# Joining the third and last layers of a graph network in one loop of fixed order, and moving half of an input check into the attention layer

## Chip, cores, metric

One core of one Trainium2 chip. The metric is device time in microseconds (us) of one execution; lower is better. Engines are PE (TensorE matmul; PEld its weight loads), DVE (VectorE), ACT (ScalarE), POOL (GpSimd) and SP (SyncE, which here only issues transfers). A name such as L935 is a line of the kernel whose profile is shown; the same statement has other line numbers in each kernel.

## The reference, cut to what matters

Four layers on 4096 nodes with 128 features, each followed by a residual sum and a layer norm. All use one 4096 x 4096 fp32 adjacency, 64 MB, of zeros and ones.

```python
x = layernorm(x + L0(x, adj, ...))   # hyperbolic graph convolution
x = layernorm(x + L1(x, adj, ...))   # attention with 4 heads, masked by adj == 0
x = layernorm(x + L2(x, adj, w2))    # relu(D^-1/2 (adj + I) D^-1/2 @ x @ w2)
x = layernorm(x + L3(x, adj, ...))   # additive attention:
#   H = X W^T + b ; e = leaky_relu(A * H a_s + A * (H a_r)^T, 0.2)
#   softmax over A > 0, times H
```

L1 is called **layer one** here and in the prediction, L2 the **third layer**, L3 the **last layer**. The change's own summary ("layer two") counts from one and means layer one by that name.

The last layer has two versions. The fast one splits exp(leaky_relu(s + r)) into factors, which is valid only if the adjacency holds nothing but 0 and 1 and the scores are not too large. So the kernel **searches** the whole adjacency for any other value: `(a != 0) != a`, summed into `odd`. A flag made from that sum chooses the branch.

## The kernel before: the parts concerned

An adjacency block `adjT[I, J]` is 1 MB (128 partitions x 2048 fp32): column tile I, row group J, NS = 8 of each. Layer one takes 32 steps (`jb`) per tile. In a step PE makes scores, ACT their exponentials, DVE masks them (`e`), and PE multiplies them by the values (`pv`) two steps later. Meanwhile pieces of the previous tile's `ending` run between the steps. ACT also reads the adjacency rows in halves, for the degrees.

```python
# layer one, rot is a pool with one buffer
def row(n):                                         # ACT issues the load of the next half row
    st["nat"] = rot.tile([P, N // 2], F32, tag="nat", name="nat")
    nc.scalar.dma_start(out=st["nat"], in_=self.adj[...])
def degree():                                       # ACT sums the half row, then loads the next
    nc.scalar.activation(nat, nat, AF.Identity, accum_out=self.deg2[:, k, i : i + 1])
    row(n + 1)
for n in range(-LEAD, len(seq)):                    # fixed order on every engine
    if n + LEAD < len(seq):
        if jb % 4 == 3 and ...: degree()
        scores(I, jb)                               # PE ps, ACT exp, DVE e
    if n >= 0:
        sums(I, jb)                                 # PE pv
        next(rest, None)                            # one piece ("bit") of the previous ending

# third layer
at2 = ctx.enter_context(tc.tile_pool(name="at2", bufs=8))
for I in range(NS):
    for J in range(NS):
        at = at2.tile([P, 4, S], F32, tag="at", name="at")
        (nc.scalar if J % 2 else nc.sync).dma_start(out=at, in_=self.adjT[I, J])
        for jb in range(4): nc.tensor.matmul(pa, lhsT=Y[:, 4 * J + jb, :], rhs=at[:, jb, :], ...)
        nc.vector.scalar_tensor_tensor(odd, at, 0.0, at, op0=ALU.not_equal, op1=ALU.not_equal,
                                       accum_out=self.odd[...])       # the search
    # product with w2, relu, residual, layer norm of the tile

# last layer: preparation (transposes, scores, row sums, flag), then the branch, then
#   exponentials, F, X + bias, and eight tiles: DVE makes w, PE multiplies F by it
```

## Time and profile before

| | us |
|---|---|
| Whole kernel, median (range of 3) | 2355.86 (2355.78 to 2356.20) |
| Layer one, start of the first pv to start of the last | 1026.8 to 1805.6 = 778.8 |
| Last pv to the third layer's first matmul (pa) | 7.8, then 8.55 of waiting after one group |
| Third layer, first to last pa | 244.5 |
| Preparation of the last layer and the branch | 50.0 |
| Last layer, first to last pa | 235.6 |

The prediction below shows the busy shares, the stretches and the chain. The waits of PE complete them (engine, its work and line, what it waited for; then us in total, how often, longest us):

```profile
PE pa L1345 <- DVE w L1342: 12.4, 1, 12.4
...
PE pa L1200 <- DMA at<-adjT: 8.6, 1, 8.6
...
PE ps L912 <- ACT e L919: 2.7, 4, 1.8
...
PE pv L938 <- DVE e L921: 1.8, 2, 1.0
```

The first line is the wait behind the branch, the second the one at the third layer's start. The last two are all that layer one's 779 us have of PE waiting: PE sets its pace.

### The profile page before, as it was taken

To read this page: it belongs to the slowest core of one execution; us is meant where nothing else is said; L and a number is where in the kernel's file an instruction comes from. 1 tells how busy PE (TensorE), PEld (TensorE's weight loads), DVE (VectorE), ACT (ScalarE), POOL (GpSimd) and SP (SyncE) were. 2 spreads that over 40 slices of the span, in tenths; PEclk is the share of its full clock that TensorE was granted. 3 is DMA by queue.
4 is the path that set the end of the run, shared out by engine and by line. 5 is a ranking of instruction groups with operands and counts; after the bars stand their busy time and mean duration, and the time that the engine had idled before them with its cause. 6 is when DMAs were issued, how large, how long until landed. Compare 5 with 4: busy or idle time off the path is not lost.

```text
span 2354.3 us, 24080 instructions
## 1 busy us (share of the span) xinstructions
PE 2013.7 (86%) x8795; PEld 1118.5 (48%) x8795; DVE 1896.6 (81%) x2708; ACT 1463.7 (62%) x1777; POOL 106.9 (5%) x146
## 2 busy tenths in 40 slices
PE   4478878777787772589999999999998999979998
PEld 4266666666665662353333333333333444444443
DVE  6488888888878788877888888888877877579887
ACT  5688898988988987558787888878875000010000
POOL 2000000000000015212000000000000000000000
PEclk7689889989888896689999999999999999979999
DMA  2455565555646450488665655556554877438884
GB/s 54 127 191 180 169 204 191 182 184 168 223 142 214 160 180 9 134 241 230 184 194 179 190 176 188 182 176 197 179 182 171 329 286 285 160 139 291 293 291 165
DMA packets 112868, 448.44 MB, mean 190 GB/s; under 512 B 9760, under 2 KB 20064, under 8 KB 71776
## 3 DMA queue, kind: packets, MB, share of 16 engines
q1 hardware_dynamic: 84944, 294.71, 36.8%
q10 hardware_dynamic: 18576, 135.27, 16.4%
q0 software_dynamic: 9216, 16.78, 4.0%
q8 instruction: 73, 1.20, 0.2%
q14 instruction: 59, 0.48, 0.1%
HBM read 369.10 MB, written 77.63 MB: 190 GB/s over the span
## 4 chain that ended last, share of the span: by engine, by line
PE 60%; DVE 21%; ACT 13%; issue 3%; DMA 2%; ACTq 0%; SPq 0%; POOL 0%; DVEq 0%; POOLq 0%
PE pv L938 16%; PE ps L912 10%; PE pa L1345 9%; PE pa L1200 9%; PE pz L583 4%; DVE w L606 3%; PE pi L674 3%; DVE t L632 3%; DVE w L636 3%; PE ptA L564 3%; ACT t L628 3%; ACT at L572 2%; ACT e L919 2%; DVE e L921 2%; ACT w L601 1%
## 5 line engine op out<-in xcount | busy, mean ns | idle before, releaser
L921 DVE SCALAR_TENSOR_TENSOR e<-at,e 128x2048 f32<-128x2048 f32 x256 | 583.2, 2288 | 131.8 <-ACT e L919 130.9
L919 ACT ACTIVATE e<-ps 128x1024 f32<-128x1024 f32 x512 | 490.8, 1025 | 144.0 <-PE ps L912 113.3
L938 PE MATMUL pv<-e,VA 128*64 128x512 f32 x2048 | 497.5, 607 | 1.8 <-DVE e L921 1.8
L912 PE MATMUL ps<-QS,KS 128*128 128x512 f32 x1024 | 312.1, 424 | 5.6 <-ACT e L919 2.7
L912 PEld LDWEIGHTS ps<-QS,KS 128*128 128x128 f32 x1024 | 172.1, 189 | 229.9 <-ACT e L919 160.4
L674 PE MATMUL pi<-HA,w 128*128 128x129 f32 x1152 | 185.9, 336 | 83.8 <-DVE w L636 83.8
L938 PEld LDWEIGHTS pv<-e,VA 128*64 128x64 f32 x2048 | 125.1, 136 | 242.4 <-issue 222.7
L1345 PE MATMUL pa<-w,F 128*128 128x512 f32 x512 | 223.5, 598 | 12.4 <-DVE w L1342 12.4
L1200 PE MATMUL pa<-at,Y 128*128 128x512 f32 x512 | 224.4, 599 | 8.6 <-DMA at<-adjT 8.6
L674 PEld LDWEIGHTS pi<-HA,w 128*128 128x128 f32 x1152 | 179.0, 249 | 94.1 <-DVE w L636 94.1
L1342 DVE SCALAR_TENSOR_TENSOR w<-rho,col,at 128x512 f32<-128x512 f32 x256 | 187.3, 747 | 19.2 <-PE pa L1345 2.0
L591 DVE SCALAR_TENSOR_TENSOR t<-ei,de,pz 128x512 f32<-128x512 f32 x144 | 107.5, 747 | 107.1 <-PE pz L583 103.3
L1210 DVE SCALAR_TENSOR_TENSOR odd<-at 128x2048 f32<-128x2048 f32 x64 | 146.6, 2291 | 42.7 <-DMA at<-adjT 39.5
L564 PE MATMUL ptA<-ident,ad 128*128 128x128 f32 x1032 | 145.3, 286 | 39.7 <-ACT at L572 32.5
L564 PEld LDWEIGHTS ptA<-ident,ad 128*128 128x128 f32 x1032 | 124.3, 148 | 96.5 <-ACT at L572 50.1
L572 ACT COPY at<-ptA 128x512 f32<-128x512 f32 x200 | 108.3, 587 | 98.7 <-PE ptA L564 98.4
L583 PE MATMUL pz<-HT 128*128 128x512 f32 x292 | 163.2, 670 | 4.5 <-DVE w L655 4.2
L1345 PEld LDWEIGHTS pa<-w,F 128*128 128x128 f32 x512 | 97.7, 192 | 134.0 <-issue 104.7
L1200 PEld LDWEIGHTS pa<-at,Y 128*128 128x128 f32 x512 | 98.0, 193 | 129.2 <-issue 127.7
L606 DVE TENSOR_TENSOR w<-w,at 128x2048 f32<-128x2048 f32 x64 | 143.8, 2283 | 0.0
L1349 ACT COPY a<-pa 128x512 f32<-128x512 f32 x8 | 4.7, 585 | 201.7 <-PE pa L1345 178.5
L642 PE MATMUL ptz<-ident,t 128*128 128x128 f32 x448 | 68.7, 294 | 67.7 <-DVE w L655 45.8
(341 smaller groups left out, 2439.9 us busy)
## 6 DMA issues: line engine op xcount, KB each, us to landing
at<-adjT SPq DMA_DIRECT2D x127, 1024.0 KB, 4.8
at<-adjT ACTq DMA_DIRECT2D x65, 1024.0 KB, 5.0
ad<-in_adj_dram SPq DMA_DIRECT2D x64, 1024.0 KB, 6.5
adjT<-at SPq DMA_DIRECT2D x64, 1024.0 KB, 8.4
nat<-in_adj_dram ACTq DMA_DIRECT2D x64, 1024.0 KB, 4.9
qk<-cut SPq DMA_DIRECT2D x16, 512.0 KB, 11.8
KS<-qk POOLq DMA_DIRECT2D x32, 256.0 KB, 8.9
QS<-qk POOLq DMA_DIRECT2D x32, 256.0 KB, 8.5
```

The lines of the kernel that those rows point to most:

```text
L564: nc.tensor.transpose(pt[:, ib, :], st[p]["ad"][k][:, ib, jb * P : (jb + 1) * P], self.ident)
L572: copy(st[p]["at"][k][:, jb, :], st[p]["pt"].pop(m))
L583: nc.tensor.matmul(pz, lhsT=HT[:, j * P : (j + 1) * P], rhs=HT[:, I * S : (I + 1) * S], start=True, stop=True)
L606: nc.vector.tensor_tensor(w, w, at, ALU.mult)
L674: nc.tensor.matmul(self.po[ib // 2][:, ib % 2, :], lhsT=w[0][:, jb, ib * P : (ib + 1) * P], rhs=HA[:, 4 * J + jb, :], start=False, stop=(J ...
L912: nc.tensor.matmul(p[:, h, :], lhsT=KS[:, h2 + h, jb * P : (jb + 1) * P], rhs=QS[I % 2][:, h2 + h, :], start=True, stop=True,)
L919: nc.scalar.activation(e[:, h2 : h2 + 2, :], p, AF.Exp)
L921: nc.vector.scalar_tensor_tensor(e, at[:, jb % 4, :].unsqueeze(1).to_broadcast([P, NH, S]), 0.0, e, op0=ALU.not_equal, op1=ALU.mult,)
L938: nc.tensor.matmul(st["po"][h // 2][g : g + 64, :], lhsT=VA[:, o : o + 64], rhs=e[:, h, :], start=(jb == 0), stop=(jb == NT - 1), skip_gro ...
L1200: nc.tensor.matmul(pa, lhsT=Y[:, 4 * J + jb, :], rhs=at[:, jb, :], start=False, stop=(J == NS - 1 and jb == 3), skip_group_check=True,)
L1342: nc.vector.scalar_tensor_tensor(w, rho[:, I * S : (I + 1) * S], col[:, 0, j : j + 1], at[:, jb, :], op0=ALU.max, op1=ALU.mult)
L1345: nc.tensor.matmul(pa, lhsT=F[:, j, :], rhs=w, start=False, stop=(j == NT - 1), skip_group_check=True)
```

## The change

The intent: PE idles in the two seams around the third layer, so both layers go into one loop. The preparation of each third-layer tile for the last layer runs beside the next tile's matmuls. The last layer's first tile, which needs only finished tiles, runs ahead of the branch. To make room on DVE, half of the search moves to layer one, where rows lie in memory anyway; these need a second row buffer, and many constants were moved to short-lived pools so that it fits. The core of the diff:

```diff
 # layer one
+            natp = ctx.enter_context(tc.tile_pool(name="natf", bufs=2))
-                    st["nat"] = rot.tile([P, N // 2], F32, tag="nat", name="nat")
+                    st["nat"] = natp.tile([P, N // 2], F32, tag="nat", name="nat")
 ... in degree():
+                st["look"] = [(nat, i, b) for b in range(2)] if k else []
+            def look():                             # one piece: 128 x 1024 on DVE
+                if st["look"]:
+                    nat, i, b = st["look"].pop(0)
+                    a = nat[:, b * N // 4 : (b + 1) * N // 4]
+                    nc.vector.scalar_tensor_tensor(a, a, 0.0, a, op0=ALU.not_equal,
+                        op1=ALU.not_equal, accum_out=self.odd[:, 2 * i + b : 2 * i + b + 1])
 ... in the loop:
                         scores(I, jb)
+                        if jb % 4 < 2:
+                            look()
 # third and last layer
-    net.layer2(w2, Y)
-    net.layer3(w3, b3, a_s, a_r, out)
+    net.layers23(w2, w3, b3, a_s, a_r, out, Y)
+            atp = pctx.enter_context(tc.tile_pool(name="at2", bufs=5))
+            w = self.load_mat(w2, "w2")             # and br, wn, ac: small loads from SP
+            def convolve(I, J): ...                 # as before, search only if J < NS // 2
+            def attend_first(J): ...                # w on DVE and PE's matmul, tile 0
+            def finish(I): ...                      # six pieces with yields: w2, norm, transposes,
+                                                    # scores, exponentials, F of tile I
+            def close_first(): ...                  # flag and column sums
+            with tc.manual_schedule():
+                nc.scalar.preload_act_table_set("natural_log_exp_and_others")
+                for g in range(BUFS):               # BUFS = 5
+                    load(g)                         # all block loads from SP
+                for g in range(groups):             # 8 * 8 + 8
+                    convolve(I, J) if I < NS else attend_first(J)
+                    ... load(g + BUFS), or the first three blocks of tile 1 ...
+                    if g == 2: weights()
+                    if J in (0, 1, 3, 5, 6): next(rest, None)
+                    if J == NS - 1 and I < NS: rest = finish(I); next(rest)
+                    if g == groups - 2: close_first()
```

## The prediction

> **What bounds the kernel now.** I read the page first (busy shares, chain), then cut the span into stages with the table of stretches, then the timeline and the chain of waits at the seams.
>
> ```profile
> PE 2013.7 (86%) x8795; PEld 1118.5 (48%) x8795; DVE 1896.6 (81%) x2708; ACT 1463.7 (62%) x1777; POOL 106.9 (5%) x146
> ```
>
> PE is the busiest engine, but 81% on DVE says that some stage may be near a second limit. The table of stretches (columns: stretch, then busy us of PE, PEld, DVE, ACT, POOL with instruction counts, then granted clock, DMA share, GB/s) for one tile of layer one (attention, lines 860 to 1062):
>
> ```profile
> 1520.00:1616.00 96.00, 95.89 (x388) 37.47 (x388) 81.04 (x92) 77.08 (x86) 2.14 (x4) 1.00 0.57 183
> ```
>
> The reader sees a stage in which PE never rests: 95.89 of 96. DVE has 15 us left per tile, ACT 19. The same table for the rest of the run, cut at the seams:
>
> ```profile
> 1806.00:1827.00 21.00, 8.41 (x26) 4.63 (x24) 13.75 (x61) 1.50 (x6) 0.00 (x0) 0.75 0.75 284
> 1827.00:2058.60 231.60, 231.34 (x616) 109.41 (x616) 174.21 (x260) 8.10 (x16) 0.00 (x0) 0.99 0.73 265
> 2058.60:2108.60 50.00, 34.01 (x197) 23.89 (x197) 35.64 (x128) 6.58 (x13) 0.00 (x0) 0.78 0.31 123
> 2108.60:2344.70 236.10, 236.10 (x580) 105.63 (x580) 208.45 (x395) 6.82 (x15) 0.00 (x0) 0.99 0.75 267
> 2344.70:2354.30 9.60, 1.26 (x9) 0.97 (x8) 4.07 (x20) 0.79 (x2) 0.00 (x0) 0.72 0.12 34
> ```
>
> Row 1 is the seam from layer one to the third layer, row 2 the third layer, row 3 the preparation of the last layer (scores, row sums, exponentials, F, bias) with the branch, row 4 the last layer, row 5 its tail. Rows 2 and 4 are pure PE: nothing done on DVE or DMA there can shorten them. The change can win only in rows 1 and 3, 71 us in all. The chain of waits says what holds these two (start us, us, what):
>
> ```profile
> 1817.98 2.83 issue
> 1821.28 5.64 DMA at<-adjT
> ...
> 2084.74 6.03 PE pm L1295 x54
> ...
> 2094.99 6.33 DVE F L1329 x32
> 2101.32 0.11 DVE F L1330
> 2101.43 4.08 DVE X L1332 x21
> ```
>
> The first transfer issued from ACT sits behind ACT's part of the last tile's ending, so the second group of the third layer lands only at 1827; and 13.6 us before the last layer are DVE building F and adding the bias, PE idle.
>
> **What the Trainium skill says.** "VectorE: DVE Perf Modes", section "The TRN2 errata", gives (N+151)/0.96 ns for an fp32 two-operand operation: 691 and 2291 ns at N = 512 and 2048. The trace has 2291 for the search (L1210) and about 0.69 apart for the w of L1342, so it agrees; for N = 1024 the formula gives 1224 ns, my estimate for one search piece. "ScalarE: Activation LUTs", section "What ACT_TABLE_LOAD costs", has 1283 ns per load; the trace shows 1.28 us (before L1323 and L171). Third-layer tiles now use Ln and Exp and need none, but ACT is idle there, so nothing comes of it. "DMA: Bandwidth & Descriptors", section "Issuing engines are not separate DMA queues", says a second issuing engine saves only issue time; an issue takes 0.32 to 0.34 us here for a megabyte needed every 3.43 us, so loading everything from SP costs nothing. "TensorE: Matmul & The Clock Gate", section "HAM oscillation", warns of idle gaps above about 3.4 us; rows 1 and 3 show it (0.75 and 0.78 granted against 0.99).
>
> **The change part by part.** *(a) Start of the third layer.* All loads go from SP and the first three buffers do not depend on the ending, so the wait before 1827 (8.6 us in the waits of PE) goes: -8.6.
>
> *(b) The preparation goes into the loop.* Of the 50.0 us of row 3, PE keeps what it must still do, at full clock: product with w2 1.2, transposes 8 x 0.58 = 4.6, row scores 8 x 0.8 = 6.4, column scores 16 records x 0.43 = 6.9, weights 1.2, the constant row 0.9: 21.2. The sum matmuls (L1295, 64) are gone; ACT's accumulation gives them. So -28.8.
>
> *(c) New stalls in the loop.* DVE and PE are in fixed order. In tiles 0 to 6 DVE has 4 x 2.33 (half of the search) plus about 8 of finishing in some 32 us, and PE waits for none of it, except once for the weights (DVE copies behind a 2.3 us search): +2. In the first tile of the last layer PE waits for w, and finishing tile 7 stands between the groups on DVE: after group 0, o 1.12 + X 0.69 + statistics 1.7 + 0.2, then the first w 0.7: 4.4; normalising 0.5; after group 5 the row and column scores on DVE (2.0) and a w: 2.4; after group 6, F, the maxima and the flag: 1.8. Sum 9.1. Branch and first w behind it: 1.2, judged from 0.8 us between the flag (2091.82) and PE's next matmul now. Together +12.3. Seams: -8.6 - 28.8 + 12.3 = **-25**.
>
> *(d) Half of the search in layer one.* 64 pieces of 128x1024, eight per tile: 8 x 1.2 = 9.8 us, DVE 81 -> 91 of 96. By shares it fits. By order it does not: the pieces come in pairs, after e of steps 8k and 8k+1, and a step's e must be ready when PE comes to its pv. The timelines of DVE and PE:
>
> ```profile
> 1627.95 2.29 DVE L921 SCALAR_TENSOR_TENSOR e<-at,e 128x2048 f32<-128x2048 f32 x1 [1.45 <-ACT e L919]
> 1630.71 2.29 DVE L921 SCALAR_TENSOR_TENSOR e<-at,e 128x2048 f32<-128x2048 f32 x1
> 1633.45 2.29 DVE L921 SCALAR_TENSOR_TENSOR e<-at,e 128x2048 f32<-128x2048 f32 x1
> 1636.21 2.29 DVE L921 SCALAR_TENSOR_TENSOR e<-at,e 128x2048 f32<-128x2048 f32 x1
> 1639.92 2.29 DVE L921 SCALAR_TENSOR_TENSOR e<-at,e 128x2048 f32<-128x2048 f32 x1 [1.35 <-ACT e L919]
> ...
> 1631.02 1.94 PE L938 MATMUL pv<-e,VA 128*64 128x512 f32 x8
> 1634.02 1.94 PE L938 MATMUL pv<-e,VA 128*64 128x512 f32 x8
> 1637.01 1.94 PE L938 MATMUL pv<-e,VA 128*64 128x512 f32 x8
> 1640.00 1.08 PE L938 MATMUL pv<-e,VA 128*64 128x512 f32 x4
> ```
>
> These are steps 7 to 10 of tile 6. e(7) starts 3.08 us before pv(7); each e takes 2.20 of DVE, and each bit of the previous tile's ending 0.55. Put two pieces of 1.25 in: e(8) starts at 2.75, e(9) at 2.75 + 2.20 + 1.25 + 0.55 = 6.75 and ends at 9.04, pv(9) is due at 9.07; e(10) starts at 6.75 + 4.0 = 10.75 and ends at 13.04, but pv(10) is due at 12.05. **PE waits 1.0.** The same for the pairs at steps 16 (bits of 0.64 and 0.42: 1.1) and 24 (0.4, with a shorter lead of 2.76: 1.0); the pair at step 0 meets no ending and fits. PE has no slack in which to make it up, so 3.1 us per tile for tiles 1 to 6 = 19, and some 2 in tile 7, whose rows come closer. Layer one: **+21**.
>
> Sum: 2355.9 - 25 + 21 = 2352; I say 2351.
>
> **The rivals.** *The search in layer one is hidden:* DVE's 15 us of free time per tile speak for it; the 2.0 us by which e(8) to e(10) are now ahead, all taken by bits and two pieces, speak against it. It would give 2331. *DVE or ACT becomes the bound of layer one:* if a piece costs 1.5, or if ACT, whose next row load must now wait for DVE to be done with a buffer, delays its exponentials, each tile loses 6 or more: 2375. For it speaks that ACT issues that load in order ahead of exponentials; against it that two row buffers leave most of a step. *The loop is held by DMA or by buffers:* five buffers instead of eight, the fourth of which may lie where the ending still works: a group takes 3.43 us of PE, and the third layer drew 265 GB/s with peaks of 426 in the DMA view, so at most some 5 us once. *The stalls of the first tile are larger*, as in (c) each is a round trip PE to DVE to PE: up to 10 more.
>
> **Range and chances.** The gain is capped: even with (d) free and half the stalls of (c), 2355.9 - 31 = 2325. The loss is capped by the same order argument: twice my stalls in (d) and 10 more in (c) give 2383, unlikely. 8 in 10 between 2328 and 2368. Faster by over 2% needs below 2308.7, more than rows 1 and 3 can give: 0.04. Slower needs above 2403: 0.03. Within 2%: 0.93.
>
> **What would show it.** Right: a tile of layer one lasts some 99 us instead of 96, PE waits for the masked e two or three times a tile for about 1 us, near steps 10, 18, 26; DVE near 91 us per tile. No wait of PE for DMA at the third layer's start; the preparation's 50 us gone, and 9 us of PE waiting for w in eight groups ahead of the branch; last layer's seven tiles still 29.5 each. Wrong: PE's tiles in layer one stay at 96 (then the time is near 2331), or PE waits for transfers in the loop, or the branch leaves more than 3 us.

## The result, and the profile after

The changed kernel takes 2352.31 us (median, 2349.25 to 2356.16, four runs) against 2356.03 for the kernel before beside it. Ratios here are the mean time of one kernel's fast runs over the mean of the other's in the same rounds, so not quite the ratio of the medians quoted. The ratio is 0.9979 (95% interval 0.9955 to 1.0002): the same. A later set of runs (e12) gave 0.9969 (0.9959 to 0.9979). All profiles quoted fell in fast runs.

The busy line of the page, then the stretches cut at the same seams (columns as in the prediction: stretch, length, busy us of PE, PEld, DVE, ACT, POOL, clock, DMA share, GB/s):

```profile
PE 2006.8 (85%) x8732; PEld 1108.2 (47%) x8732; DVE 1892.2 (81%) x2760; ACT 1491.7 (64%) x1830; POOL 107.2 (5%) x146
```

```profile
1813.50:1833.10 19.60, 3.88 (x21) 2.66 (x17) 12.37 (x62) 1.85 (x7) 0.00 (x0) 0.59 0.31 105
1833.10:2084.70 251.60, 250.92 (x730) 123.22 (x731) 131.87 (x280) 37.55 (x71) 0.00 (x0) 0.99 0.75 275
2084.70:2130.50 45.80, 37.12 (x93) 16.38 (x91) 31.23 (x67) 6.02 (x12) 0.00 (x0) 0.93 0.50 194
2130.50:2338.00 207.50, 207.50 (x517) 92.79 (x516) 181.47 (x360) 6.24 (x14) 0.00 (x0) 0.99 0.77 272
```

They are the seam, the third layer, the first tile of the last layer with the branch, and its other seven tiles. The preparation of 50 us is gone, but the seam has not become shorter. The waits of PE:

```profile
PE pa L1287 <- DMA at<-adjT: 11.6, 1, 11.6
PE pa L1310 <- DVE w L1307: 8.0, 3, 4.5
...
PE pv L952 <- DVE e L935: 7.1, 22, 1.0
...
PE ps L926 <- ACT e L933: 2.4, 3, 2.1
```

Line 1 is new in size: 11.6 us of waiting for the third layer's first blocks, where the prediction had none. Line 2 was expected as 9.1 us. Line 3 answers to the 1.8 us of before.

| step | predicted | measured | how |
|---|---|---|---|
| (a) last pv to a running third layer | -8.6 | +1.8 | see next paragraph |
| (b) + (c) preparation into the loop, new stalls | -16.5 | -16.0 | rest of the way to the last pa |
| (d) layer one | +21 | +7.5 | 786.3 (1027.2 to 1813.5) against 778.8 |
| sum | -4 | -6.7 | spans 2354.3 and 2348.3 differ by 6.0 |

For (a): before, 21.5 us from the last pv until the wait ends at 1827.06, with one group of matmuls done meanwhile, which takes 3.7 us at full clock (235.6 us of the last layer / 64 groups): 21.5 - 3.7 = 17.8. After: 19.6, with none done. For (b) + (c): from the last pv to the last pa it is 538.6 us before and 524.4 after, so -14.2; less the +1.8 of (a), -16.0.

The sum was predicted to 3 us, but (a) and (d) were each off by more than 10 us, in opposite directions. The rest of this document is about these two.

**What stands at the third layer's start.** The timelines of PE and of SP's queue in the changed kernel, and the waits of SP:

```profile
1812.14 1.94 PE L952 MATMUL pv<-e,VA 128*64 128x512 f32 x8 [1.03 <-DVE e L935]
1814.01 1.44 PE L975 MATMUL pto<-ident,ev 128*128 128x128 f32 x8
1819.41 2.05 PE L1281 MATMUL pa<-ident,Y 128*128 128x128 f32 x8 [3.96 <-DVE junk L993]
1833.09 12.80 PE L1287 MATMUL pa<-at,Y 128*128 128x512 f32 x24 [11.63 <-DMA at<-adjT]
```

```profile
1815.41 0.33 SPq L81 DMA_DIRECT2D br<-in_L_gnn_b_dram  x1
...
1818.51 0.43 SPq L1235 DMA_DIRECT2D ac<-in_L_gnn_b_dram  x1
1827.05 19.19 SPq L1271 DMA_DIRECT2D at<-adjT  x8
```

```profile
SPq L1271 <- DVE X L1026: 7.9, 1, 7.9
```

The small loads go out up to 1818.9, so SP is free. The first block load (L1271) then waits until 1827.05 for DVE's X at L1026, which is the layer norm of layer one's last tile, and the block lands 6 us later. None of that data is needed by the load. So it should be memory that it waits for, since the buffers of `at2` lie where layer one's pools lay; e1 tests this.

**What happens in layer one.** DVE and PE around steps 7 to 10 of a tile; to be read beside the lines of the prediction:

```profile
1535.28 2.29 DVE L935 SCALAR_TENSOR_TENSOR e<-at,e 128x2048 f32<-128x2048 f32 x1 [0.88 <-ACT e L933]
1538.04 2.29 DVE L935 SCALAR_TENSOR_TENSOR e<-at,e 128x2048 f32<-128x2048 f32 x1
1540.24 1.22 DVE L916 SCALAR_TENSOR_TENSOR nat<-nat 128x1024 f32<-128x1024 f32 x1
...
1541.93 2.29 DVE L935 SCALAR_TENSOR_TENSOR e<-at,e 128x2048 f32<-128x2048 f32 x1
1544.14 1.22 DVE L916 SCALAR_TENSOR_TENSOR nat<-nat 128x1024 f32<-128x1024 f32 x1
...
1545.83 2.29 DVE L935 SCALAR_TENSOR_TENSOR e<-at,e 128x2048 f32<-128x2048 f32 x1
```

```profile
1538.93 1.94 PE L952 MATMUL pv<-e,VA 128*64 128x512 f32 x8
...
1548.17 1.94 PE L952 MATMUL pv<-e,VA 128*64 128x512 f32 x8 [0.19 <-DVE e L935]
```

The picture is the predicted one, two pieces between e(8), e(9) and e(10), and PE stalls at pv(10). But the stall is 0.19 us, not 1.0. One reason is a number the prediction read from the old trace: e(7) now starts 3.65 us before pv(7) (1535.28, 1538.93), not 3.08. ACT shows why. First before, then after the change, at the same place of a tile (ACTq is ACT's issue of a transfer; brackets give the idle time before an instruction):

```profile
1625.31 0.20 ACT L904 ACTIVATION_READ_ACCUMULATOR nat<-nat 128x1 f32 x1
1625.54 0.33 ACTq L896 DMA_DIRECT2D nat<-in_adj_dram  x1
1625.98 3.77 ACT L919 ACTIVATE e<-ps 128x1024 f32<-128x1024 f32 x4 [0.47 <-DVE e L921]
```

```profile
1530.06 0.33 ACTq L899 DMA_DIRECT2D nat<-in_adj_dram  x1
...
1533.22 0.20 ACT L907 ACTIVATION_READ_ACCUMULATOR nat<-nat 128x1 f32 x1
1533.31 1.94 ACT L933 ACTIVATE e<-ps 128x1024 f32<-128x1024 f32 x2
```

With one row buffer the load of the next half row must wait for the end of the sum that reads the buffer, and ACT, which issues it, stands 0.47 us before its next exponential. With two, the load at this place goes out before the sum and the gap is gone. That holds for every second load only. The others go into the buffer that has been searched; they still go out behind the sum, and in the tile from 1508 to 1607 ACT stands 0.75, 0.47, 0.47 and 1.14 us there. The last of the four is the longest because it also waits for DVE: the sum ends at 1594.08, the piece of search at 1594.74, and the load goes out at 1594.77.

```profile
1594.66 0.08 DVE L916 DVE_READ_ACCUMULATOR nat<-nat 128x1 f32 x1
...
1593.88 0.20 ACT L907 ACTIVATION_READ_ACCUMULATOR nat<-nat 128x1 f32 x1
1594.77 0.33 ACTq L899 DMA_DIRECT2D nat<-in_adj_dram  x1
1595.21 3.77 ACT L933 ACTIVATE e<-ps 128x1024 f32<-128x1024 f32 x4 [1.14 <-DVE Y L1035]
```

### The profile page after: what moved, and what is told of

The parts are those of the page before. It is cut to its first block, busy times and chain, and to the rows that moved or that the text cites. A ratio compares the mean times of both kernels' runs of the same rounds, so it can differ in the third digit from the quotient of the medians.

```text
span 2348.3 us, 24024 instructions
## 1 busy us (share of the span) xinstructions
PE 2006.8 (85%) x8732; PEld 1108.2 (47%) x8732; DVE 1892.2 (81%) x2760; ACT 1491.7 (64%) x1830; POOL 107.2 (5%) x146
## 4 chain that ended last, share of the span: by engine, by line
PE 49%; DVE 30%; ACT 15%; issue 5%; DMA 2%; ACTq 0%; POOL 0%; SPq 0%; DVEq 0%; POOLq 0%
PE pa L1287 9%; PE pv L952 9%; PE pa L1471 8%; DVE e L935 8%; PE ps L926 5%; PE pz L585 5%; ACT e L933 4%; PE pi L676 3%; DVE w L608 3%; DVE w L638 3%; PE ptA L566 3%; DVE t L634 3%; ACT t L630 3%; DVE nat L916 2%; ACT at L574 2%
## 5 line engine op out<-in xcount | busy, mean ns | idle before, releaser
L1287 PE MATMUL pa<-at,Y 128*128 128x512 f32 x512 | 227.0, 597 | 11.6 <-DMA at<-adjT 11.6
L1471 PE MATMUL pa<-w,F 128*128 128x512 f32 x448 | 197.0, 598 | 0.0
L585 PE MATMUL pz<-HT 128*128 128x512 f32 x292 | 168.2, 688 | 4.3 <-DVE w L657 3.8
L1468 DVE SCALAR_TENSOR_TENSOR w<-rho,col,at 128x512 f32<-128x512 f32 x212 | 154.0, 746 | 20.0 <-PE pa L1471 8.1
L1471 PEld LDWEIGHTS pa<-w,F 128*128 128x128 f32 x448 | 84.2, 191 | 107.2 <-issue 79.8
L907 ACT ACTIVATE nat<-nat 128x2048 f32<-128x2048 f32 x64 | 122.6, 1916 | 3.8 <-DMA nat<-in_adj_dram 3.8
L695 PEld LDWEIGHTS pj<-HA,w 128*128 128x128 f32 x896 | 104.5, 191 | 13.2 <-issue 12.9
```

The lines of the kernel that those rows point to most:

```text
L585: nc.tensor.matmul(pz, lhsT=HT[:, j * P : (j + 1) * P], rhs=HT[:, I * S : (I + 1) * S], start=True, stop=True)
L1287: nc.tensor.matmul(st["pa"], lhsT=Y[:, 4 * J + jb, :], rhs=at[:, jb, :], start=False, stop=(J == NS - 1 and jb == 3), skip_group_check=True,)
L1468: nc.vector.scalar_tensor_tensor(w, rho[:, I * S : (I + 1) * S], col[:, 0, j : j + 1], at[:, jb, :], op0=ALU.max, op1=ALU.mult)
L1471: nc.tensor.matmul(pa, lhsT=F[:, j, :], rhs=w, start=False, stop=(j == NT - 1), skip_group_check=True)
```

## Theories to test

*Mine, formed after the result.* (1) The seam is lost to the place of the buffers, not to the transfers. (2) The search costs layer one close to what was predicted, by its order on DVE. The second row buffer that comes with it gives back about half. (3) The stalls of the first tile are order, too.

*Rivals.* (1') The blocks are late because SP must first issue the small loads. (2') The search is mostly hidden (7.5 us is its whole cost), and the kernel before had no other loss in layer one. (3') DVE is full in the first tile, so a stall taken away there comes back one group later.

## Experiments

All were correct and checked for races. The ratios are to the kernel before on the same chip, with the 95% interval. "pv" is the stretch from first to last pv.

### e1: the pools of layer one in another order

```diff
-            rot  = ...(name="rotf", bufs=1)
-            natp = ...(name="natf", bufs=2)
-            atp  = ...(name="atf", bufs=1)
-            ep   = ...(name="ef", bufs=3)
+            ep   = ...(name="ef", bufs=3)
+            natp = ...(name="natf", bufs=2)
+            atp  = ...(name="atf", bufs=1)
+            rot  = ...(name="rotf", bufs=1)
```

> The changed kernel with one edit: in layer one's attention the pool with the ending's small tiles is opened last, so that the fused loop's five load buffers no longer lie on it. Theory (in the changed kernel the first load of the third layer waits until 1827.05 us for the end of the ending, because one buffer of its pool overlaps those tiles and the wait is taken for the pool as a whole): the first load goes out about 8 us earlier, right after the small weight loads (1819), the first third-layer matmul at about 1825 instead of 1833.1, total 2349 to 2340. Rival (PE's own start, the transfer's latency or a jump to new instructions holds it): the first matmul stays near 1833, total unchanged.

Measured: 2346.8 us, 0.9949 (0.9932 to 0.9965). Waits of PE, and SP's queue:

```profile
PE pa L1287 <- DMA at<-adjT: 3.6, 1, 3.6
```

```profile
1822.19 0.43 SPq L1235 DMA_DIRECT2D ac<-in_L_gnn_b_dram  x1
1822.86 3.03 SPq L1271 DMA_DIRECT2D at<-adjT  x5
```

The first block now goes out right behind the last small load, and the seam falls from 19.6 to 11.6 us. Nothing was changed but which tiles lie where, so (1) holds for 8.0 of the 10.4 us that separate +1.8 from -8.6. The 3.6 us that stay may be the small loads ahead of the blocks (1'); e9 moves these. Of the 8 us the third layer gave 3.4 back (254.5 us from first to last pa against 251.1), all of it in its first tile. 1.0 of it is PE's longer wait for the weights (1.7 us against 0.7), which now meets DVE's backlog of search (see e11); another 1.7 are the 40 matmuls behind that wait, which take 19.03 us for 17.33, at a granted clock of 0.51 in the first 3.5 us; the rest is in the three groups before it (13.39 us for 12.80). Layer one itself was 1.8 us longer (788.1), and PE waits 5.2 us for score buffers there, against 2.4; why was not tested.

### e2: the whole search back in the loop, two row buffers kept

```diff
-                        if jb % 4 < 2:
-                            look()                  # and the other calls of look()
-                if J < NS // 2:                     # in convolve
+                if J < NS:
```

> The changed kernel with the whole search in the fused loop, none in layer one. Theory (the search costs PE about 1.2 us per tile of layer one by order on VectorE, and nothing in the fused loop, where no matmul waits for it): a layer-one tile from 98.4 back to 97.2, 7.5 to 8.5 us off in all; the third layer's stretch stays within 2 us; total 7 us lower, about 2342. Rival (VectorE, with 4 x 2.33 us more per tile, holds the fused loop or its buffers): the third layer's stretch grows by 8 us or more and the total does not fall.

Measured: 2335.04 us, 0.9910 (0.9894 to 0.9927), twice the expected gain. pv takes 769.2 us: 17.1 less than in the changed kernel, but also 9.6 less than before the change, which (2') can't explain. The third layer takes 251.3 us, as with half of the search (251.1): the loop had room for all of it, and moving it out of there bought nothing.

### e3: no bit of an ending in a step that has a piece of search

```diff
                         if jb % 4 < 2 and st["look"]:
                             look()
+                            looked = True
                         sums(I, jb)
-                        next(rest, None)
+                        if not looked:
+                            next(rest, None)
```

> The changed kernel, but no bit of the previous tile's ending is put on VectorE in a step that has a search piece. Same work on every engine, another order. Theory (PE waits for e only where two search pieces and the ending's bits meet in three steps): the three stalls per tile (0.2 to 0.4 us idle, 1.2 us of period) go, a tile from 98.4 to 97.3, total 7 us lower. Rival (the stage is longer because VectorE's share is near its end, 91 of 98 us, or because of contention for memory): the tile stays at 98.4.

Measured: 2342.16 us, 0.9933 (0.9917 to 0.9950). The same pieces run in layer one, in the same places, but pv takes 776.7 us and a tile 96.82:

```profile
PE ps L926 <- ACT e L933: 3.6, 2, 2.2
PE pv L952 <- DVE e L935: 1.8, 2, 1.0
```

Against 7.1 us in 22 waits, PE waits twice for e in this stage, the second time at the layer's end as every kernel here does. So it is the order, not DVE's share of time, that makes the search cost most of what it costs in a full tile. What is left of it (776.7 against 769.2 in e2) is, by the starts of pv, 0.2 us in each of six tiles and 6.3 us in the last tile, whose rows come closer together (see e10).

### e6: half of the search in layer one, added to the kernel before

The kernel before plus the second row buffer, `look()` as in the change, and `if J < NS // 2` in its own third layer; one small pool was divided to make room.

> The kernel before, with only half of the search moved into layer one (two row buffers, pieces as in the change) and half left in the third layer; third and last layer stay as before. Theory: layer one longer by 8 us as in the changed kernel (tile 97.2 to 98.4), the third layer no shorter (231.6 us, PE bound), total about 2364. Rival from my prediction's arithmetic (21 us in layer one): about 2377. Rival (the search on VectorE was holding the third layer): that stretch shrinks and the total is at or below 2356.

Measured: 2365.18 us, 1.0036 (1.0026 to 1.0047). pv takes 785.4 us, as in the change, and the third layer 244.0 against 244.5: taking half the search from a stage that PE bounds gains nothing. So part (d) by itself costs 8.5 us (6.1 to 11.1), of which pv shows 6.6.

### e10: only the second row buffer, added to the kernel before

```diff
+            natp = ctx.enter_context(tc.tile_pool(name="natf", bufs=2))
-                    st["nat"] = rot.tile([P, N // 2], F32, tag="nat", name="nat")
+                    st["nat"] = natp.tile([P, N // 2], F32, tag="nat", name="nat")
```

> The kernel before with nothing changed but a second buffer for the rows that ACT reads (and one small pool divided so that it fits). Theory: the second buffer itself gives layer one some 9 us, which hides half of the cost of the search there: first to last pv 769 us as in e2 instead of 779, tile period 96.6 instead of 97.2, total 2346 to 2348 against 2356. Rival: layer one was PE-bound before and the buffer changes nothing: total 2355 to 2357; then the 9.6 us that e2 is under the kernel before must come from something else in the change.

Measured: 2349.72 us, 0.9958 (0.9945 to 0.9971), 9.9 us less. One tile of layer one, in the kernel before, in e10, and in the changed kernel (stretches as above, each from one use of the queries' buffer to the next):

```profile
1503.23:1600.44 97.21, 97.09 (x394) 37.76 (x392) 82.25 (x92) 78.09 (x89) 2.14 (x4) 1.00 0.57 184
```

```profile
1507.92:1604.52 96.60, 96.60 (x394) 37.90 (x392) 82.72 (x92) 77.97 (x90) 2.14 (x5) 1.00 0.57 185
```

```profile
1409.64:1508.07 98.43, 97.60 (x394) 37.64 (x392) 91.05 (x108) 78.11 (x90) 2.15 (x5) 1.00 0.56 182
```

A tile shrinks from 97.21 to 96.60 us with one more buffer, and grows to 98.43 with the search. Note that the first line looks saturated, 97.09 of 97.21 busy, for the same 394 matmul records that take 96.60 in the second: short waits hide inside the records. The bigger part is at the end: from 1600.44 to the last pv at 1805.6 it is 205.2 us before, and from 1604.52 to 1803.4 in e10 198.9. pv in all is 769.1 us. So the buffer gives 9.7 us. The search costs 17.1 (changed kernel against e2) or 16.3 (e6 against e10, which differ in little else), and 7.5 is the difference of 17.1 and the 9.6 that e2 is under the kernel before. (2) holds in its sizes; its cause, the order on DVE, does not cover the whole cost.

Where the search costs, the starts of pv show, step by step, the changed kernel against e10. In a full tile it is 1.83 us: 0.27, 0.30 and 0.81 near steps 10, 18 and 26, the places of the prediction, and 0.23 and 0.19 near steps 2 and 22. The row load that goes out late near step 26 costs PE nothing of its own: e ends at 1597.34 there, and pv starts at 1597.39. In the last tile it is 6.1 us, 4.0 of them in two steps (2.4 and 1.6) where the rows come closer together. The kernel before has these two long steps as well (2.2 and 1.5 us over e10, of the 5.7 us that e10 gains in that tile): ACT waits there for rows that have not landed. The waits of ACT in the changed kernel's layer one:

```profile
ACT nat L907 <- DMA nat<-in_adj_dram: 3.8, 3, 2.3
```

Before the change this wait is 4.3 us, in 5 cases; with two buffers and no search (e10, e2) there is none. So in the last tile the search takes back what the second buffer gave there, probably because it holds the buffer longer; no run tests that by itself.

### e4: ACT's lead taken away again

```diff
                 nc.scalar.activation(nat, nat, AF.Identity, accum_out=self.deg2[:, k, i : i + 1])
+                if k:
+                    nc.scalar.copy(pad, nat[:, 0:576])      # 0.57 us of ACT
```

> The changed kernel with an ACT copy of some 0.57 us put after every second row half, which delays the exponentials of the next step so that the masked e starts about 3.1 us ahead of its pv as before the change, instead of 3.65. Theory (each of the three stalls is the deficit that my sum gave, less the 0.57 of lead that the second row buffer added): stalls at steps 10, 18 and 26 grow to about 0.8 to 1.0 each, 3 per tile, some +10 us in all: 2360 to 2364. Rival (the lead doesn't matter, the stalls are set by DVE's order alone): 2351 to 2354.

Measured: 2365.01 us, 1.0033 (1.0021 to 1.0045); pv takes 801.5 us, 15.2 more than in the changed kernel. DVE and PE at the same steps, and the waits of PE:

```profile
1542.52 2.29 DVE L938 SCALAR_TENSOR_TENSOR e<-at,e 128x2048 f32<-128x2048 f32 x1 [1.60 <-ACT e L936]
```

```profile
1545.44 1.94 PE L955 MATMUL pv<-e,VA 128*64 128x512 f32 x8
...
1555.40 1.94 PE L955 MATMUL pv<-e,VA 128*64 128x512 f32 x8 [0.83 <-DVE e L938]
```

```profile
PE pv L955 <- DVE e L938: 15.7, 21, 1.7
PE ps L929 <- ACT e L936: 8.4, 10, 1.8
```

The lead is 2.92 us and the stall at pv(10) 0.83 us, against 3.65 and 0.19. The direction and size of the stalls are as the theory says (0.75 on average, 15.7 / 21, for the 0.8 to 1.0 expected). Layer one grew by 15.2 us where some 10 were expected (the whole lies 1 us above the range), and the copies also make PE wait for score buffers (8.4 us against 2.4), which was not foreseen.

### e7: w one group ahead in the first tile of the last layer

```diff
-            wp = pctx.enter_context(tc.tile_pool(name="w2", bufs=4))
+            wp = pctx.enter_context(tc.tile_pool(name="w2", bufs=8))
+                    if g == groups - NS - 1: make(0)          # w of the next group on DVE,
+                    if I == NS and J < NS - 2: make(J + 1)    # ahead of the finishing piece
 ... make(NS - 1) inside close_first, behind the transposes ...
```

> The changed kernel with the w of the last layer's first tile made one group ahead of PE, in front of the piece of finishing work on DVE, with eight w buffers instead of four. Theory: the 8.0 us in which PE waits for w in the first tile are order and not work, so they fall to about 2 (only the branch's part stays): total 2346 to 2348 against the changed kernel's 2352, first tile 40 us instead of 45.8. Rival: DVE is full there, and the wait comes back a group later: no change.

Measured: 2339.61 us, 0.9906 (0.9883 to 0.9929). By the stages, the first tile and branch take 35.6 us instead of 45.8; the other stages are those of the changed kernel within 1 us. Waits of PE:

```profile
PE pa L1313 <- DVE w L1304: 1.1, 1, 1.1
```

The waits fell by 6.9 us, the stage by 10.2. The difference is the clock. Two stretches of the changed kernel, right after its waits of 4.53 and 2.22 us, and all of e7's first tile (the third number from the right is the granted clock):

```profile
2093.70:2097.00 3.30, 3.30 (x4) 1.50 (x5) 3.30 (x8) 1.03 (x2) 0.00 (x0) 0.50 0.19 22
...
2117.20:2122.50 5.30, 5.30 (x9) 2.16 (x10) 3.33 (x12) 0.00 (x0) 0.00 (x0) 0.68 0.00 0
```

```profile
2087.30:2122.90 35.60, 33.74 (x93) 15.01 (x91) 28.47 (x65) 6.02 (x12) 0.00 (x0) 1.00 0.59 235
```

3.30 us at 0.50 lose 1.65 us and 5.30 at 0.68 lose 1.70, 3.35 together: 6.9 + 3.35 = 10.2. (3) holds, (3') falls, and each of the two longer stalls cost about 1.7 us more than its own length in this profile. The 1.1 us wait of e7 cost no clock. The price is not fixed: with the same two waits, the 24 and 8 matmuls behind them (10.5 and 3.6 to 3.7 us where no clock is lost) take 12.22 and 5.40 us in the changed kernel, 12.87 and 5.40 in e1, but 13.53 and 3.70 in e2, where the wait of 2.22 us cost no clock. The medians of whole runs fell by some 11 to 13 us and e7's four runs spread over 10.8 us, so the stages are the firmer measure.

### e9: four edits together

The edits of e1, e2 and e7, and the small loads issued after the first two blocks instead of before them.

> The changed kernel with four edits together: the tile pools of layer one opened in the other order (as e1), the small loads of the last layer behind the first two groups of the third layer, w made a group ahead (as e7), and the whole search left in the third layer's loop (as e2). Theory that the pieces add up: 2352 - 17 - 8 - 3 - 5 = 2319, 2315 to 2325; first pa some 9 us after the last pv. Rival: the pieces share the same slack and the sum falls short: 2326 to 2332.

Measured: 2319.70 us, 0.9826 (0.9807 to 0.9844). The gains add up to the 2319 expected. The third layer's first pa comes 7.7 us after the last pv (11.6 in e1), and PE waits only 0.9 us for a block afterwards: the small loads ahead of the blocks had been worth about 4 us, so (1') has a part in it. (The run has four edits, but e2 and e7 by themselves left the seam at 19.1 and 18.9 us.) A new wait of 6.7 us appeared, for the weights of the last layer behind three queued pieces of search.

### e11: the weights at group 6 instead of 2

```diff
-                    if g == 2:
+                    if g == 6:
                         weights()
```

> The kernel of e9 with one number changed: the weights of the last layer are prepared in group 6 of the third layer instead of group 2. In e9 PE waited 6.7 us there for a copy that stood on DVE behind three pieces of search that had queued up. Theory: by group 6 DVE (2.4 us of search in a group of 3.4 us of PE) has caught up, the wait falls to at most 2.3 us: 2315 against 2320 for e9 on its own chip, ratio to the kernel before about 0.9805. Rival: DVE is behind for the whole first tile and the wait only moves: 0.9826 as e9.

Measured: 2313.67 us, 0.9814 (0.9791 to 0.9837). The wait is 1.4 us, under the 2.3 allowed for:

```profile
PE pw L1249 <- DVE last L1248: 1.4, 1, 1.4
```

This is the best version found, 44 us under the kernel before and some 37 under the changed one beside it (e12). Whether it is over 2% faster than the kernel before, the interval leaves open.

### e12: the changed kernel again

> The changed kernel itself, unedited, on this chip, as the partner of e11 and as a second measurement of the change: ratio to the kernel before 0.9965 to 0.9995, layer one from first to last pv 786 us, seam 19.6 us, first tile and branch 45.8 us. If it came below 0.995, the cancelling of two errors that I read from the first pair of traces would be a matter of that chip.

Measured: 2350.87 us, 0.9969 (0.9959 to 0.9979). pv takes 786.1 us, PE's wait for blocks is 11.2 us and for w 8.0. The stages repeat in a later run, so the two cancelling errors are not a matter of one trace.

## Why the prediction came out right, point by point

The total (2351 for 2352.3) was right partly by luck: two steps failed by 10.4 and 13.5 us and nearly cancelled. Within (d), two more errors of opposite sign lie hidden.

- **(a) Start of the third layer: failed.** The step said "the first three buffers do not depend on the ending, so the wait before 1827 goes: -8.6". The first load waited all the same (7.9 us on DVE X). By reckoning from the pools, only one of the five buffers overlaps a tile of the ending; no trace shows addresses. Moving the pools so that none should overlap moved the first load forward (e1), so the wait came from where the buffers lay. The third rival had named the buffer, but priced it at 5 us as a wait of the fourth load. The small loads ahead of the blocks were left out too; e9 shows what they cost, about 4 us (11.6 to 7.7).
- **(b) The preparation goes into the loop: right.** Of its 50 us, (b) + (c) left 34.0 (50.0 - 16.0). Of these, 9.4 are visible waits (8.0 for w, 0.7 for the weights, 0.7 at the branch) and 3.35 the clock behind the two longer ones. The 21.3 that remain, by difference, are what PE still does; the count was 21.2.
- **(c) New stalls: right.** The three waits for w, 4.53, 2.22 and 1.21 us, stand against 4.4, 2.4 and 1.8; a fourth, of 0.5, did not come. The branch and the weights cost 0.7 us each, under the 3.2 allowed for both. The clock after a stall was left out; it fills the gap: 9.4 + 3.35 = 12.8 against 12.3.
- **(d) Half the search in layer one: the places right, the sizes off.** The step predicted +21 and the layer grew by 7.5. It failed in these terms. First, it took the second row buffer as free of effect, where it gains 9.7 us (e10): before the change ACT stood 0.47 us behind each row load. Second, the three stalls of a full tile cost 1.4 us together (1.8 us with all else in the tile), not 3.1, since that same buffer gives e a lead of 3.65 us over pv. Third, the last tile costs 6.1 us, not "some 2": ACT waits for rows there (e10). With these two the search costs some 17 us, which looks close to 21 only because one term was too high and the other too low. The prediction's own sum with the measured numbers (lead 3.65; e(8) to e(9) 3.89 us apart, 1538.04 to 1541.93) gives e(10) at 2.75 + 2 x 3.89 + 2.29 = 12.82 against pv(10) due at 12.62: a stall of 0.20, measured 0.19; the spacing of e is measured too, so this tests only that PE waits for the end of e. With the lead taken back the stalls return (e4). In the tile, DVE is busy 91.05 us, as predicted. The tile takes 98.4 for "some 99", but the prediction had read the tile of the kernel before as 96, the length of the stretch that it had cut; it was 97.21, so the tile grew by 1.2 and not by 3.
- **Rivals.** "Hidden" falls with e2, and with e6 against e10. "DVE or ACT becomes the bound" falls with e3: same share, other order, no stalls. The fear that ACT's row load would have to wait for DVE came true once in a full tile (near step 26, a gap of 1.14 us, at no cost to PE), and perhaps, by the late rows, in the last tile. At every second load the second buffer made ACT wait less instead.
- **A side remark was wrong.** "Third-layer tiles now use Ln and Exp and need none": they need two table loads per tile, 16 in all, of 1.28 us each (L1336 and L1337), probably because the preload (L1396) went out at 0.74 us, at the start of the program. ACT has the time, so no stage shows it; that was not tested by itself.

What stays open: whether the first use of a pool always waits for everything under all of its buffers, or only did here. e1 shows that removing one overlap frees the first load, no more.

## What to carry to other kernels

When a change needs another buffer, price the buffer by itself: it moves the transfer's issue, and with it the engine that issues. Count too what reads the buffer last, since the next transfer waits for it. Add work between two engines in fixed order by its place, not by its share: write down when each consumer is due, and put a new piece only where no other extra stands. And at a seam between two stages, look at where the next stage's first buffers lie, since a load that depends on no data may still wait for the last tile's memory.

## What the Trainium skill lacked or had wrong

- "DMA: Bandwidth & Descriptors", section "Issuing engines are not separate DMA queues", gives the time to initiate a transfer as all there is to save. It lacks the wait ahead of it: an engine that issues a load stands until the load's buffer is free. Here that was a gap of 0.47 us in ACT at a row load; with it, and with the rows that came late in the last tile, layer one took 9.7 us longer (e10).
- "TensorE: Matmul & The Clock Gate", section "HAM oscillation", ties the lower clock to idle gaps above about 3.4 us. Here a wait of 2.22 us, behind a stretch of small products, was already followed by 0.68 over 5.3 us, and one of 1.69 us (e1, the weights) by 0.51 over 3.5 us, while 1.1 us (e7) and 1.4 us (e11) cost nothing. In e2 the wait of 2.22 us cost nothing either, so no threshold comes out of these runs.
- No page read for this case says that the first load into a new pool can wait for the work that still uses the memory under it; here it did, for 7.9 us, and the order in which older pools were opened decided it (e1).
